# A selective scan in a four-layer network: products written over the states, inputs loaded four units ahead, and doubled pieces one unit earlier

## The chip, the cores and the metric

The kernel runs on one core of a Trainium2 chip. The metric is the device time of one execution in microseconds; the median of some runs is compared. A difference of a few tenths of a per cent is near the limit of what such a comparison can tell.

## What is computed

The network has four layers, each added to its input: a deformable convolution, an edge filter with a 1x1 convolution, a two-way WKV recurrence, and a selective state-space layer (Mamba-like). The change is in the last one. Cut to what matters, for x of 2 x 192 x 96 x 96 (L = 9216 positions), 384 channels d and 16 states n:

```python
x_in, z = split(x_norm @ W_in.T)                 # 384 channels each
u = silu(causal_conv4(x_in) + conv_b)
dt, B, C = split(W_x @ u)                        # 12, 16, 16 rows
delta = softplus(W_dt @ dt + 2 * b_dt)
for t in range(L):                               # for each channel d and state n
    h = exp(delta[t] * A) * h + (delta[t] * u[t]) * B[t]
    y[t] = sum_n(h * C[t])
out = x + W_out @ ((y + D * u) * silu(z))
```

## The kernel before

The last layer is `layer3`. It cuts the 9216 positions of each of the two images into steps ("stages" here): 17 of 511 positions and two of 265 and 264, which are the first two of the first image and the last two of the second. So there are 38 stages. A stage is 12 units, numbered q = 0 to 11; a unit k is a quarter of 128 channels, and its four tiles of 128 partitions hold 8 channels x 16 states each. Everything is float32.

A unit goes through these steps, each a nested function:

- `load` (L2441): SyncE's DMA brings delta * u of the unit's channels, spread over the 16 states, from a DRAM tile `ud` into a buffer `bu` of 128 x 4 x 512. There are four such buffers. `start_of` (L2449, ScalarE) writes the state from the unit's last stage into column 0.
- `times_b` (L2456, GpSimd) multiplies `bu` by B, in place.
- `steps_of` (L2466, TensorE) spreads delta over the states into PSUM banks `da`, of which there are five; `decay` (L2480, ScalarE) takes the four exponentials in place.
- `scan` (L2489, VectorE) runs four scans over the positions, from `da` and `bu` into a tile `h` (three buffers).
- `keep` (L2496, ScalarE) saves the last column of `h`.
- `times_c` (L2513, VectorE) multiplies three of the four tiles of `h` by C, which is in PSUM, into a tile `hc`; `times_c_aside` (L2524, GpSimd) does the fourth into `hp`. Both have three buffers.
- `sum_of` (L2537, TensorE) sums over the states into a bank `acc`; the first unit of each four starts it with `skip` (L2531). After four units `gate` (L2550, VectorE) multiplies by silu(z).

The rest of the work for other stages is cut into pieces by generators, and the loop calls `go` to run the next piece: `early` for the stage after next (21 pieces: two of loading and normalizing; then the six projections, L2344, and three convolutions, L2364, each one piece on TensorE and one copy or activation on ScalarE; then the silu), `late` for the next stage (B, C, delta and the stores to `ud`, L2427, after GpSimd's `du`, L2425) and `output` for the one before. All their matmuls write one PSUM bank, `pe`.

The order on TensorE, VectorE, ScalarE and GpSimd is as written in the loop; SyncE's DMAs are put in order by the scheduler. Within unit k the order is: if q is in `AHEAD`, two pieces; the sum of unit k-2; the scan of k; the load of k+3; the decay matmuls of k+1; one piece of `BEHIND`; the exponentials of k+1; another piece; the product with C; GpSimd's product with C of unit k-1 and its product with B of unit k+2; the first column of k+3; the saved column of k. The tables that say where pieces stand:

```python
AHEAD = {1: "late", 7: "early", 8: "early", 9: "early"}
BEHIND = {0: "late", 1: "late", 2: "late", 3: "out", 4: "out", 5: "early", 6: "early",
          7: "early", 8: "early", 9: "early", 10: "early"}
```

Two or one further pieces are run in units 3, 4, 5, 6, 7 and 11.

Of the kernel before, what the change touches and what calls it, by code (L numbers as in the profile page):

```python
# [6 lines left out]
F32 = mybir.dt.float32  # L7
I32 = mybir.dt.int32
AF = mybir.ActivationFunctionType
ALU = mybir.AluOpType  # L10
# [8 lines left out]
P = 128  # L19
# [44 lines left out]
class Net:  # L64
# [2113 lines left out]
    def layer3(self, x, out, stats):  # L2178
# [3 lines left out]
        nc, tc, ins = self.nc, self.tc, self.ins  # L2182
        TM = 511
# [8 lines left out]
        with ExitStack() as ctx:  # L2192
            wp = ctx.enter_context(tc.tile_pool(name="w3", bufs=1))
            s1 = ctx.enter_context(tc.tile_pool(name="l3s", bufs=1))
            sb = ctx.enter_context(tc.tile_pool(name="l3", bufs=2))
            s3 = ctx.enter_context(tc.tile_pool(name="l3h", bufs=3))
            sc = ctx.enter_context(tc.tile_pool(name="l3c", bufs=4))
            dr = ctx.enter_context(tc.tile_pool(name="l3d", bufs=2, space=DRAM))
# [100 lines left out]
            steps = []  # L2299
# [6 lines left out]
            got = {}  # L2306
# [126 lines left out]
            def where(k):  # L2433
                return k // NQ, k % NQ, k % NQ // NV, k % NV

            def load(k):
                s, q, i, v = where(k)
                T = steps[s][2]
                t = sc.tile([P, 4, TM + 1], F32, name="bu")[:, :, : T + 1]
                one = got[s]["ud"][i, v]  # L2440
                nc.sync.dma_start(  # L2441
                    out=t[:, :, 1:],
                    in_=bass.AP(one.tensor, one.offset, [[0, NST], [4 * T, 8], [1, 4 * T]]),
                )
                got[s]["bu", q] = t

            def start_of(k):
                s, q, _, _ = where(k)
                nc.scalar.copy(  # L2449
                    got[s]["bu", q][:, :, 0], none if steps[s][1] == 0 else state[:, q]  # L2450
                )
# [24 lines left out]
            def decay(k):  # L2476
                s, q, _, _ = where(k)
                for r in range(4):
                    da = got[s]["da", q][r][:, 1:]
                    nc.scalar.activation(  # L2480
                        da, da, AF.Exp, scale=nA[:, 4 * q + r : 4 * q + r + 1]
                    )

            def scan(k):
                s, q, _, _ = where(k)
                h = s3.tile([P, 4, TM + 1], F32, name="h")[:, :, : steps[s][2] + 1]
                bu = got[s]["bu", q]
                for r in range(4):
                    nc.vector.tensor_tensor_scan(  # L2489
                        h[:, r], got[s]["da", q][r], bu[:, r], 0.0, ALU.mult, ALU.add  # L2490
                    )
                got[s]["h", q] = h
# [5 lines left out]
            def rows_c(s):  # L2498
                cc = ps.tile([P, TM], F32, name="cc")[:, : steps[s][2]]
                nc.tensor.matmul(  # L2500
                    cc,
                    pick.rearrange("p n e -> p (n e)"),
                    got[s]["xd"][:NST],
                    start=True,
                    stop=True,
                )
                got[s]["cc"] = cc

            def times_c(k):
                s, q, _, _ = where(k)  # L2510
                T = steps[s][2]
                hc = s3.tile([P, 3, TM], F32, name="hc")[:, :, :T]
                nc.vector.tensor_tensor(  # L2513
                    hc,
                    got[s]["h", q][:, :3, 1:],
                    got[s]["cc"].unsqueeze(1).to_broadcast([P, 3, T]),
                    ALU.mult,
                )
                got[s]["hc", q] = hc

            def times_c_aside(k):
                s, q, _, _ = where(k)
                hp = s3.tile([P, TM], F32, name="hp")[:, : steps[s][2]]
                nc.gpsimd.tensor_tensor(hp, got[s]["h", q][:, 3, 1:], got[s]["cs"], ALU.mult)  # L2524
                got[s]["hp", q] = hp

            def sum_of(k):
                s, q, i, v = where(k)
                if v == 0:
                    acc = ps.tile([P, TM], F32, name="acc")[:, : steps[s][2]]  # L2530
                    nc.tensor.matmul(  # L2531
                        acc, skip[:, i], got[s]["us"][:, i], start=True, stop=False
                    )
                    got[s]["acc"] = acc
                acc = got[s]["acc"]
                for r in range(4):
                    nc.tensor.matmul(  # L2537
                        acc[32 * r : 32 * r + 32],
                        gather[:, v],
                        got[s]["hc", q][:, r] if r < 3 else got[s]["hp", q],  # L2540
                        start=False,
                        stop=v == NV - 1,
                        tile_position=(0, 32 * r),
                    )

            def gate(k):
                s, q, i, v = where(k)
                if i == 0:
                    got[s]["y"] = s1.tile([P, ND, TM], F32, name="y")[:, :, : steps[s][2]]
                nc.vector.tensor_tensor(  # L2550
                    got[s]["y"][:, i], got[s]["acc"], got[s]["zs"][:, i], ALU.mult
                )

            def output(s):
                b, t0, T = steps[s]
                y = got[s]["y"]
                xr = s1.tile([CH, 2, TM], F32, name="xr")[:, :, :T]
                nc.sync.dma_start(out=xr, in_=halves(x[b])[:, :, t0 : t0 + T])
                for m in range(2):
                    pe = bank(T)  # L2560
                    for d in range(ND):
                        nc.tensor.matmul(
                            pe[:CH],
                            w_out[:, d, m * CH : (m + 1) * CH],
                            y[:, d],
                            start=d == 0,
                            stop=d == ND - 1,
                        )
                    yield
                    nc.vector.tensor_tensor(xr[:, m], pe[:CH], xr[:, m], ALU.add)  # L2570
                    if m == 1:
                        nc.sync.dma_start(out=halves(out[b])[:, :, t0 : t0 + T], in_=xr)
                    yield
# [4 lines left out]
                        pass  # L2578
            spare.clear()
            nk = ns * NQ  # L2580
            for k in range(3):
                load(k)
                start_of(k)
            for k in range(2):
# [1 line left out]
            rows_c(0)  # L2586
            steps_of(0)
            decay(0)
            AHEAD = {1: "late", 7: "early", 8: "early", 9: "early"}
            BEHIND = {  # L2590
                0: "late",
                1: "late",
# [12 lines left out]
            def go(name):  # L2605
                next(running[name], None)

            for k in range(nk):
                s, q, _, _ = where(k)
                if q == 0 and s + 1 < ns:  # L2610
                    running["late"] = late(s + 1)
                if q == 2 and s:
                    running["out"] = output(s - 1)
                if q == 3 and s + 2 < ns:
                    running["early"] = early(s + 2)
                if q in AHEAD:
                    go(AHEAD[q])
                    go(AHEAD[q])
                if k >= 2:
                    sum_of(k - 2)  # L2620
                if q == 0 and s:
                    rows_c(s)
                scan(k)
                if k + 3 < nk:
                    load(k + 3)
                if q in (4, 5):
                    go("out")
                if k + 1 < nk:
                    steps_of(k + 1)
                if q in BEHIND:  # L2630
                    go(BEHIND[q])
                if k + 1 < nk:
                    decay(k + 1)
                if q in BEHIND and BEHIND[q] != "out":
                    go(BEHIND[q])
                if q == 3:
                    go("late")
                    go("early")
                    go("late")
                times_c(k)  # L2640
                if q == 4:
                    go("late")
                if k >= 2 and (k - 2) % NV == NV - 1:
                    gate(k - 2)
                if q in (6, 7):
                    go("late")
                if q in (4, 11):
                    go("early")
                if k:
                    times_c_aside(k - 1)  # L2650
                if k + 2 < nk:
                    times_b(k + 2)
                if q == 4:
                    go("late")
                if k + 3 < nk:
                    start_of(k + 3)
                keep(k)
            sum_of(nk - 2)
            times_c_aside(nk - 1)
# [97 lines left out]
```

## Time and profile before

| | |
|---|---|
| median of 3 runs | 10140.82 us (10130.94 to 10147.6) |
| profiled execution | 10135.06 us, its span 10133.3 us |
| last layer's scans | from 7009.46 us to the end |
| busy from 7143 to 10040 us (2897 us) | TensorE 2666, VectorE 2701, ScalarE 1860, GpSimd 2664 us |
| granted TensorE clock, DMA engines' busy share there | 0.91, 0.80 (177 GB/s) |

Times in the profile are microseconds unless marked ns. A group's row gives the line, the engine, the operation, output and inputs by the program's names, shapes, the number, then the busy time and the mean ns of one, then the idle time of the engine just before them and what ended it. A row of waits gives who waited for whom, the total, the number and the longest. PE is TensorE, DVE VectorE, ACT ScalarE, POOL GpSimd, SP SyncE. A float32 matmul stands as two records.

### The profile page before, as it was taken

To read this page: it belongs to the slowest core of one execution; us is meant where nothing else is said; L and a number is where in the kernel's file an instruction comes from. 1 tells how busy PE (TensorE), PEld (TensorE's weight loads), DVE (VectorE), ACT (ScalarE), POOL (GpSimd) and SP (SyncE) were. 2 spreads that over 40 slices of the span, in tenths; PEclk is the share of its full clock that TensorE was granted. 3 is DMA by queue.
4 is the path that set the end of the run, shared out by engine and by line. 5 is a ranking of instruction groups with operands and counts; after the bars stand their busy time and mean duration, and the time that the engine had idled before them with its cause. 6 is when DMAs were issued, how large, how long until landed. Compare 5 with 4: busy or idle time off the path is not lost. (4 is left out here: it accounts for less than half of the span.)

```text
span 10133.3 us, 222497 instructions
## 1 busy us (share of the span) xinstructions
PE 9017.0 (89%) x87686; PEld 5301.1 (52%) x87686; DVE 8276.5 (82%) x8874; ACT 6078.5 (60%) x11850; POOL 7002.5 (69%) x5653
## 2 busy tenths in 40 slices
PE   4799999999979999999979777787999999999998
PEld 3578878877768877788853222223222222222223
DVE  5788878888768887777756789885899999999998
ACT  0366666666657766677721169664666666666665
POOL 1466676666666666666630258774899999999998
PEclk8899999999989999999989888987999999999998
DMA  8455555555424455455545344443788878788876
GB/s 147 96 135 136 140 135 138 136 136 135 126 72 136 137 144 143 138 137 139 137 117 159 122 141 164 125 128 80 173 178 180 178 178 180 178 178 176 180 177 150
DMA packets 878318, 1465.18 MB, mean 145 GB/s; under 512 B 251745, under 2 KB 682405, under 8 KB 877189
## 3 DMA queue, kind: packets, MB, share of 16 engines
q1 hardware_dynamic: 663276, 1264.09, 49.1%
q0 software_dynamic: 105152, 133.19, 5.7%
q10 hardware_dynamic: 108840, 53.57, 2.1%
q8 instruction: 701, 11.49, 0.5%
q14 instruction: 349, 2.85, 0.1%
HBM read 871.06 MB, written 381.46 MB: 124 GB/s over the span
## 5 line engine op out<-in xcount | busy, mean ns | idle before, releaser
L616 DVE TENSOR_TENSOR sp<-h 128x2304 f32<-128x2304 f32 x790 | 2183.5, 2796 | 34.4 <-ACT h L595 34.4
L2489 DVE TENSOR_TENSOR_SCAN h<-da,bu 128x512 f32<-128x512 f32 (+2 forms) x1824 | 1981.2, 1147 | 239.7 <-ACT da L2480 189.7
L2456 POOL TENSOR_TENSOR bu<-bu,bs 128x2044 f32<-128x2044 f32 (+2 forms) x456 | 1960.0, 4298 | 175.9 <-DMA bu<-ud 127.9
L640 ACT COPY st<-pt 128x512 f32<-128x512 f32 (+1 forms) x2370 | 1214.0, 515 | 1090.0 <-PE pt L632 1017.8
L632 PE MATMUL pt<-ident,sp 128*128 128x128 f32 x14220 | 1677.0, 276 | 84.0 <-DVE sp L616 39.0
L638 DVE COPY st<-pt 128x512 f32<-128x512 f32 x1580 | 1060.3, 687 | 760.2 <-PE pt L632 748.4
L632 PEld LDWEIGHTS pt<-ident,sp 128*128 128x128 f32 x14220 | 1567.9, 142 | 166.1 <-issue 95.5
L586 POOL TENSOR_TENSOR h<-u,step 128x1152 f32<-128x1152 f32 (+1 forms) x474 | 1106.9, 2354 | 628.5 <-DVE u L559 436.9
L604 POOL DMA_DIRECT2D xw<-xp_d x2500 | 1391.0, 619 | 153.9 <-PE pt L683 53.4
L2480 ACT ACTIVATE da<-da,nA 128x511 f32<-128x511 f32 (+2 forms) x1824 | 1063.6, 639 | 583.2 <-PE da L2466 577.2
L683 PE MATMUL pt<-st,xw 64*32 64x288 f32 (+1 forms) x30000 | 1107.7, 370 | 169.1 <-DVE st L638 92.1
L709 ACT COPY val<-pt 128x288 f32<-128x288 f32 (+1 forms) x3000 | 958.7, 404 | 306.3 <-PE pt L683 285.6
L811 PEld LDWEIGHTS pf<-main,wd 126*64 126x64 f32 x17064 | 913.9, 140 | 155.6 <-issue 148.4
L811 PE MATMUL pf<-main,wd 126*64 126x128 f32 (+1 forms) x17064 | 986.5, 274 | 9.6 <-DMA far_m<-val 9.2
L2466 PE MATMUL da<-dl,spread 32*128 32x511 f32 (+2 forms) x3648 | 888.2, 650 | 17.5 <-DVE h L2489 17.4
L683 PEld LDWEIGHTS pt<-st,xw 64*32 64x32 f32 x30000 | 547.7, 106 | 594.7 <-DVE st L638 167.6
L2513 DVE TENSOR_TENSOR hc<-h,cc 128x1533 f32<-128x1533 f32 (+2 forms) x456 | 750.7, 1646 | 0.0
L832 PE MATMUL pf<-more,wl 118*64 118x144 f32 (+5 forms) x11592 | 732.9, 277 | 2.5 <-DMA more<-far_l 2.4
L832 PEld LDWEIGHTS pf<-more,wl 118*64 118x64 f32 (+1 forms) x11592 | 665.7, 137 | 69.7 <-issue 62.7
L2466 PEld LDWEIGHTS da<-dl,spread 32*128 32x128 f32 x3648 | 281.2, 194 | 599.7 <-DVE h L2489 370.2
L2524 POOL TENSOR_TENSOR hp<-h,cs 128x511 f32<-128x511 f32 (+2 forms) x456 | 552.7, 1212 | 47.5 <-DVE h L2489 35.6
L2344 PE MATMUL pe<-xn,sb_w_in 96*128 96x511 f32 (+2 forms) x864 | 479.7, 683 | 91.5 <-ACT zs L2359 38.7
(360 smaller groups left out, 13089.2 us busy)
## 6 DMA issues: line engine op xcount, KB each, us to landing
bu<-ud SPq DMA_DIRECT2D x408, 1022.0 KB
main<-val SPq DMA_DIRECT2D x2016, 91.1 KB
far_l<-val SPq DMA_DIRECT2D x288, 324.0 KB
xw<-xp_d POOLq DMA_DIRECT2D x2500, 26.0 KB, 3.1
far_m<-val SPq DMA_DIRECT2D x288, 162.0 KB
half_d<-hv SPq DMA_DIRECT2D x54, 768.0 KB
hv<-half_d SPq DMA_DIRECT2D x54, 768.0 KB
more<-far_l SPq DMA_DIRECT2D x576, 60.8 KB
```

The source lines that it names most:

```text
L586: nc.gpsimd.tensor_tensor(hs, u[:, :, 8 * KK * l : 8 * KK * l + n].unsqueeze(3).to_broadcast([P, 2, n, WS]), con["step"].unsqueeze(1).unsq ...
L604: nc.gpsimd.dma_start(out=xw[e * WN : (e + 1) * WN, i], in_=xp_d[y : y + WS, x : x + WS, e * CM // 2 : e * CM // 2 + XW],)
L616: nc.vector.tensor_tensor(sp.rearrange("p s (y x) -> p s y x", x=WS), hy.unsqueeze(3).to_broadcast([P, n, WS, WS]), hx.unsqueeze(2).to_bro ...
L632: nc.tensor.transpose(pt[:, q], sp[:, 2 * (q0 + q) : 2 * (q0 + q) + 2].rearrange("p e w -> p (e w)"), self.ident,)
L640: nc.scalar.copy(st[:, q0 : q0 + m], pt[:, :m])
L683: nc.tensor.matmul(to, xw[e * WN : (e + 1) * WN, win, g * CG : g * CG + 32], sts[pair][e * WN : (e + 1) * WN].rearrange("p s (r c) -> p s ...
L811: nc.tensor.matmul(place(cv, m, 2 - t // 3, 2 - t % 3, None, 0), con["wd"][:, cv, t, m * CO : (m + 1) * CO], blocks(took, 1, rows), start= ...
L832: nc.tensor.matmul(place(cv, m, 2 * cv if alone else 1 - cv, 2 - t, h, 1 - alone,), con["wl"][lanes, slot, t, m * CO : (m + 1) * CO], bloc ...
L2456: nc.gpsimd.tensor_tensor(bu, bu, got[s]["bs"].unsqueeze(1).to_broadcast([P, 4, steps[s][2]]), ALU.mult)
L2466: nc.tensor.matmul(das[r][:, 1:], spread[at, v].rearrange("p n e -> p (n e)"), got[s]["dl"][at, i], start=True, stop=True, tile_position=( ...
L2480: nc.scalar.activation(da, da, AF.Exp, scale=nA[:, 4 * q + r : 4 * q + r + 1])
L2489: nc.vector.tensor_tensor_scan(h[:, r], got[s]["da", q][r], bu[:, r], 0.0, ALU.mult, ALU.add)
```

## The change

Three edits in `layer3`:

- Both products with C are written over the states in `h`: column t of the output takes the place of column t of a row whose states stand in columns 1 to T, so each product is shifted by one. `hc` and `hp` are gone, the sum reads `h`, and `h` has four buffers instead of three.
- `bu` has five buffers instead of four, in a pool of its own; the load and the first column of unit k+4, not k+3, are issued in unit k, and four instead of three are issued before the loop.
- The two pieces ahead of the sum stand in units 6, 7 and 8 instead of 7, 8 and 9.

Lines below the new pool's are numbered one higher, those below the products fewer by one.

```diff
+            s5 = ctx.enter_context(tc.tile_pool(name="l3b", bufs=5))
...
-                t = sc.tile([P, 4, TM + 1], F32, name="bu")[:, :, : T + 1]
+                t = s5.tile([P, 4, TM + 1], F32, name="bu")[:, :, : T + 1]
...
-                h = s3.tile([P, 4, TM + 1], F32, name="h")[:, :, : steps[s][2] + 1]
+                h = sc.tile([P, 4, TM + 1], F32, name="h")[:, :, : steps[s][2] + 1]
...
             def times_c(k):
-                hc = s3.tile([P, 3, TM], F32, name="hc")[:, :, :T]
+                h = got[s]["h", q]
                 nc.vector.tensor_tensor(
-                    hc,
-                    got[s]["h", q][:, :3, 1:],
+                    h[:, :3, :T],
+                    h[:, :3, 1:],
                     got[s]["cc"].unsqueeze(1).to_broadcast([P, 3, T]),
                     ALU.mult,
                 )
-                got[s]["hc", q] = hc
 
             def times_c_aside(k):
-                hp = s3.tile([P, TM], F32, name="hp")[:, : steps[s][2]]
-                nc.gpsimd.tensor_tensor(hp, got[s]["h", q][:, 3, 1:], got[s]["cs"], ALU.mult)
-                got[s]["hp", q] = hp
+                h = got[s]["h", q][:, 3]
+                nc.gpsimd.tensor_tensor(h[:, : steps[s][2]], h[:, 1:], got[s]["cs"], ALU.mult)
...
-                        got[s]["hc", q][:, r] if r < 3 else got[s]["hp", q],
+                        got[s]["h", q][:, r, : steps[s][2]],
...
-            for k in range(3):
+            for k in range(4):
                 load(k)
                 start_of(k)
...
-            AHEAD = {1: "late", 7: "early", 8: "early", 9: "early"}
+            AHEAD = {1: "late", 6: "early", 7: "early", 8: "early"}
...
-                if k + 3 < nk:
-                    load(k + 3)
+                if k + 4 < nk:
+                    load(k + 4)
...
-                if k + 3 < nk:
-                    start_of(k + 3)
+                if k + 4 < nk:
+                    start_of(k + 4)
```

## The prediction

> Units of a stage are counted 0 to 11 here (q in the code), so the title's units seven to nine are q = 6, 7, 8. "Pieces" are the steps of the generators `early`, `late` and `output`; piece 5 is the second projection of `early`.
>
> **What bounds the kernel now.** I read first the page's groups, then one full stage (units 0 to 11 whose first scan starts at 8586.94 us; the next stage's starts at 8671.68, so it took 84.74 us), grouped by shape on VectorE and GpSimd:
>
> ```profile
> L2489 DVE TENSOR_TENSOR_SCAN h<-da,bu 128x512 f32<-128x512 f32 x48 | 54.7, 1202 | 4.8 <-ACT da L2480 4.7
> L2513 DVE TENSOR_TENSOR hc<-h,cc 128x1533 f32<-128x1533 f32 x13 | 22.5, 1728 | 0.0
> L2550 DVE TENSOR_TENSOR y<-acc,zs 128x511 f32<-128x511 f32 x3 | 2.0, 682 | 0.8 <-PE acc L2537 0.8
> L2456 POOL TENSOR_TENSOR bu<-bu,bs 128x2044 f32<-128x2044 f32 x12 | 54.2, 4515 | 4.6 <-DMA bu<-ud 4.6
> ```
>
> VectorE idles only 4.8 + 0.8 = 5.6 us in the stage, and nearly all of it waits for the decays (`da`), which TensorE and ScalarE make; GpSimd idles 4.6 us for the loads of `bu`. The products with C wait for nothing (0.0). Over the whole layer the table of waits says how much of GpSimd's lateness reaches VectorE:
>
> ```profile
> DVE h L2489 <- ACT da L2480: 189.7, 174, 22.5
> POOL bu L2456 <- DMA bu<-ud: 119.4, 68, 5.7
> DVE h L2489 <- POOL bu L2456: 42.9, 26, 4.8
> ```
>
> So 119.4 us of load waits become at most 42.9 us on the path. What makes the decays late is read from the chain of waits between 8620 and 8700 us, which is units 5 to 9 of that stage (start, length, what):
>
> ```profile
> 8627.69 3.75 PE pe L2344 x4
> 8631.44 1.70 PE acc L2531 x2
> 8633.14 1.24 PE acc L2537 x8
> 8634.38 1.11 PE da L2466 x8
> 8635.49 2.37 ACT da L2480 x4
> 8637.86 0.52 ACT xi L2352
> 8638.43 1.99 PE pe L2344 x4
> ...
> 8649.53 2.37 ACT da L2480 x4
> 8651.90 0.53 ACT zs L2359
> 8652.43 0.04 issue
> 8652.47 3.69 PE pe L2364 x8
> 8656.17 0.99 PE acc L2537 x8
> ```
>
> From 8627.69 on the chain is TensorE and ScalarE, no longer VectorE. A doubled piece is a link of its own: its matmul uses the one bank `pe`, so it waits for the copy of the piece before it (8637.86), and that copy stands behind the four exponentials. Note the first row: four matmuls in 3.75 us, while the same four take 1.99 later. The table of stretches tells why (length, TensorE busy, granted clock, then DMA):
>
> ```profile
> 8626.79:8630.20 3.41, 2.85 (x4) 0.50 0.49 128
> 8630.21:8633.61 3.40, 3.40 (x8) 0.50 0.83 216
> 8633.63:8637.03 3.40, 3.40 (x20) 1.00 0.33 75
> 8456.13:8459.53 3.40, 2.73 (x9) 1.00 0.41 120
> 8459.55:8462.95 3.40, 3.40 (x5) 0.50 0.74 187
> 8462.96:8466.36 3.40, 3.40 (x19) 1.00 0.82 206
> ```
>
> The clock is at half in unit 5 of each stage and changes only on a grid of 3.41 us. A half-clock stretch that TensorE filled (3.40) was followed by full clock, here and in another stage at 8459.55; one with 0.56 us of idle (2.85) was followed by a second half-clock stretch.
>
> **The change, part by part.**
>
> *Products written over the states.* The same 12 products a stage on VectorE, the same 12 on GpSimd, same shapes; two pools go. An in-place product with a PSUM operand stands in the trace: `xr` (L2570), 655 ns for 511 columns, against 682 ns for `y` (L2550), which is not in place. GpSimd's product with B (L2456) is in place: 4515 ns for 2044, 1129 for 511, against 1266 for `hp` today. So I take 0. Bounds: 12 x -0.03 = -0.3 us a stage; upward the in-place L2419, 2.09 us for the 1533 elements of a 1.73 us product, a different operation: +0.36 us x 12 = +4.3 us. It also adds no wait: the state saved by ScalarE is the column T, which no product overwrites, and `h` gets a fourth buffer, so the scan of unit k overwrites unit k-4, whose sum TensorE issued two units before. The waits that go (for `hc` and `hp` buffers) cost 0.0 today.
>
> *Five buffers, loads four ahead.* A load is still released by the scan of unit k-1, but it is for unit k+4, so it has one unit (6.1 us or more) longer to land. It stays one place behind on SyncE's queue relative to the `ud` stores: today units 10 and 11 wait there behind the store that waits for GpSimd's `du`, after the change only 11. GpSimd's waits at the products of units 10 and 11 (1.53, 1.91 and 0.19 us here, longest 5.7) go. On the path that is between 0 and the 42.9 us above; but where unit 11 was late, the wait of 1.41 us in the next unit 1 (the silu and its table loads) shrank: 42.9 - 26 x 1.41 = 6. I take 6 to 12, about 0.3 us a stage. Cover: GpSimd's own work, 79 us a stage, must stay below the stage; it does.
>
> *Doubled pieces one unit earlier.* All 21 pieces of `early` stay; those of units 6 to 8 move. Today the doubled ones are the projections 7 and 11 and the convolution 15 (L2364, 3.69); afterwards the projections 5, 9 and 13.
> Removed: in unit 9 the convolution follows the decay matmuls at once, without waiting for exponentials and copy: 2.37 + 0.53 + 0.04 = 2.94 us off the chain.
> Added: in unit 6 TensorE, done with the first projection at 8631.44, must wait for its copy (end 8632.11, start 8632.15: 0.71 us, as in 8637.86 to 8638.43) and then do piece 5 ahead of the sums and the decay matmuls for unit 7. VectorE has no slack there: unit 7's scan waits for its decay already. Two prices:
> - clock back at 8633.62 as today: piece 5 does 1.47 us at half and 0.98 at full rate, 2.45; the skip and sum after it now run at full rate (0.86 + 0.99 for 1.70 + 1.24, -1.09). 0.71 + 2.45 - 1.09 = 2.07, net -0.87 us a stage.
> - half clock for one stretch more: piece 5 takes 4 x 0.855 = 3.42, the skip 1.70, the sum 0.99 (-0.25): 0.71 + 3.42 - 0.25 = 3.88, net +0.94 us.
> The stretch 8630.21 to 8633.61 gets an idle of 0.71; it would be busy for 2.7 us, less than the 2.85 after which the clock stayed at half. So I take the second price for a stage that lies like this one, and the first where the grid falls so that one stretch holds all of the first projection.
>
> The Trainium skill, "TensorE: Matmul & The Clock Gate", section "HAM oscillation — how this bites in real kernels", says that idle gaps are harmless below about 3.4 us. By that rule the 0.71 us costs no clock, and the sum would be the first price in every stage, 10103 us. This trace differs from it: the idle of the stretch at 8626.79 is 0.56 us, and the clock was at half for it and the next one. [...]
>
> **The sum.** 33 full stages lie between 7142.77 and 9949.52: 85.05 us each, of which I put 0.3 to late loads. A stage like this one goes to 84.74 + 0.94 = 85.7, one with the clock back early to 83.9. Which of them comes is set by the grid: 25 of its steps are 25 x 3.413 = 85.33 us. Unit 5's half clock began at 8541.46, 8626.79, 8712.13, 8797.46 and 8882.79, always 85.33 apart though the stages differ. A stage of 85.7 slides 0.4 us against the grid each time until the early case comes, and one of 83.9 slides back; the mean settles near 85.33. 33 x (85.33 - 85.05) = +9 us. The four half-length stages I leave at 0 (at the prices of a full stage, 4 x -0.87 to 4 x +0.94). The profiled execution is 10135.06 us (span 10133.3 and 1.8 around it), so it becomes 10144; the median of the three runs lies 5.8 above it: 10150. That is no change: 0.2% (20 us) is about what a measurement of this kernel can tell.
>
> **Rivals.**
> *Faster, the clock comes back in time.* The 0.7 us does not hold the clock down. Then every full stage is near 83.9: 33 x 1.15 = -38, 10103. For it: other idle gaps, 1.06 us each in units 7 to 9, leave the clock at 1.0. Against it: those begin at full clock, and the one row that begins at half with a gap stayed at half.
> *Slower, unit 6 is the new late unit.* The half clock holds for one stretch more in every full stage and nothing slides back: 85.7 to 86.1 (late loads unchanged), 33 x 0.65 to 1.05 = +21 to +35, 10162 to 10176. It decides if in nearly every stage unit 7's scan starts over 9.5 us after unit 6's (6.50 here). An in-place product at L2419's price would add to it: in units 0 to 6, where VectorE is the bound, 7 x 0.36 x 33 = +83.
> *It does nothing on the path:* loads early, products the same, links exchanged at par: 10141, inside the forecast's case.
>
> **How the numbers follow.** No change, 0.37: the grid's mean and the exchange at par. Faster 0.31: it needs a clock that recovers, or late loads at more than I take; low end 10085, the early clock with 18 of the 42.9 us on top. Slower 0.32: the extra stretch; the high end, 10190, is the slower case with a part of the in-place bound. The forecast's own range is 10121 to 10161.
>
> **What would show it.** Right: no wait of L2457 for `bu`; scan before unit 7 waiting about 3 us for `da`, none before 10 and 11; the gap before the gate gone; half-clock stretches in unit 5 reaching 10.2 us; stages near 85.3. Wrong: L2514 above 1.75 us (in-place price), unit 7 waiting below 2.3 us (clock back), or TensorE no longer on the chain in units 7 to 9.

## The result, and the profile after

| | before | after |
|---|---|---|
| median | 10141.74 us (10128.45 to 10154.08, 18 runs) | 10160.17 us (10142.56 to 10166.25, 18 runs) |
| ratio after / before | | 1.0016, 95% interval 1.0009 to 1.0022 |
| profiled execution, its span | 10135.06, 10133.3 us | 10163.15, 10161.2 us |
| first scan of the last layer | 7009.46 us | 7020.69 us |
| first scan to the end of the span | 3123.83 us | 3140.55 us |
| mean of the 33 full stages | 85.05 us | 85.51 us |

The forecast was 10150 us and no change beyond 0.2%. The time is 18 us longer by the medians, 0.16%, with an interval whose upper end just passes 0.2%. It is a near thing: the forecast's own range ends at 10161, and 8 of the 18 runs lie above that. The two profiled executions differ by 28 us, but 11.2 of these lie before the layer's first scan, where of the change only the fourth load stands (over all kernels of this case that point lies between 7000.8 and 7020.7 us). The layer itself is 16.7 us longer, 33 x 0.46 = 15.2 of it in full stages.

The same groups as before, for the stage that starts at 8609.29 us and takes 85.50 us (output and inputs, shapes, number, busy us, mean ns, idle before and what ended it):

```profile
L2490 DVE TENSOR_TENSOR_SCAN h<-da,bu 128x512 f32<-128x512 f32 x49 | 56.0, 1203 | 7.0 <-ACT da L2481 7.0
L2514 DVE TENSOR_TENSOR h<-h,cc 128x1533 f32<-128x1533 f32 x13 | 22.5, 1727 | 0.0
L2549 DVE TENSOR_TENSOR y<-acc,zs 128x511 f32<-128x511 f32 x3 | 2.0, 683 | 0.0
L2420 DVE SCALAR_TENSOR_TENSOR du<-ln,du 128x1533 f32<-128x1533 f32 x1 | 1.7, 1747 | 0.0
...
L2457 POOL TENSOR_TENSOR bu<-bu,bs 128x2044 f32<-128x2044 f32 x12 | 54.2, 4518 | 1.2 <-DMA bu<-ud 1.2
```

The in-place product takes 1727 ns (1728 before): no price. The gap before the gate is gone (0.8 to 0.0), and GpSimd's wait for loads is down from 4.6 to 1.2. VectorE's wait for the decays grew from 4.7 to 7.0. Over the layer the waits say the same:

```profile
DVE h L2490 <- ACT da L2481: 283.8, 166, 22.6
...
POOL ln L2422 <- DVE du L2420: 137.2, 34, 4.3
...
POOL bu L2457 <- DMA bu<-ud: 59.2, 34, 7.0
...
DVE h L2490 <- POOL bu L2457: 14.9, 8, 4.5
```

VectorE waits 94 us more for `da` (283.8 against 189.7) and 28 us less for `bu` (14.9 against 42.9). The chain of waits of the same stage shows where the new wait is made (start, length, what; units 5 to 7):

```profile
8649.40 3.76 PE pe L2345 x4
8653.16 0.02 issue
8653.18 0.02 ACTq L2353
8653.20 0.04 issue
8653.24 0.59 ACT xi L2353
8653.83 0.04 issue
8653.88 3.78 PE pe L2345 x4
8657.65 1.29 PE acc L2530 x2
8658.94 0.99 PE acc L2536 x8
8659.94 1.11 PE da L2467 x8
8661.05 2.37 ACT da L2481 x4
```

TensorE ends the first projection at 8653.16, waits 0.72 us for its copy, and then does the second one in 3.78 us, all at half clock. And the table of stretches (length, then the busy time of TensorE, its weight loads, VectorE, ScalarE and GpSimd, each with its number of instructions, then granted clock, DMA share and GB/s):

```profile
8648.16:8651.57 3.41, 3.18 (x5) 1.17 (x4) 3.41 (x5) 0.82 (x2) 3.41 (x2) 0.50 0.52 136
8651.58:8654.98 3.40, 2.67 (x4) 0.59 (x3) 3.40 (x4) 0.78 (x3) 3.40 (x2) 0.50 0.90 216
8654.99:8658.40 3.41, 3.41 (x6) 1.25 (x4) 2.64 (x2) 0.58 (x1) 3.41 (x3) 0.50 0.43 100
8658.41:8661.81 3.40, 3.40 (x20) 0.96 (x19) 0.02 (x1) 0.78 (x2) 3.40 (x1) 1.00 0.02 3
```

The stretch with the gap (2.67 busy of 3.40) was followed by a third one at half clock; that one was filled (3.41), and the clock came back. Unit 5's half clock is 10.24 us long in 32 of the 33 full stages (6.83 in 24 of them before), and from stage 5 to 26, counted from 0, it begins every 85.33 us: 8562.83, 8648.16, 8733.50, 8818.83. These are 25 steps of the 3.41 us on which the clock changes (the grid). A stage whose length stays at a whole number of such steps is called locked below.

### The profile page after: what moved, and what is told of

The parts are those of the page before. It is cut to its first block, busy times and chain, and to the rows that moved or that the text cites. A ratio compares the mean times of both kernels' runs of the same rounds, so it can differ in the third digit from the quotient of the medians.

```text
span 10161.2 us, 221966 instructions
## 1 busy us (share of the span) xinstructions
PE 9094.1 (89%) x87686; PEld 5330.0 (52%) x87686; DVE 8244.7 (81%) x8874; ACT 6084.1 (60%) x11850; POOL 6984.1 (69%) x5653
## 5 line engine op out<-in xcount | busy, mean ns | idle before, releaser
L2490 DVE TENSOR_TENSOR_SCAN h<-da,bu 128x512 f32<-128x512 f32 (+2 forms) x1824 | 1981.5, 1148 | 307.4 <-ACT da L2481 283.8
L2457 POOL TENSOR_TENSOR bu<-bu,bs 128x2044 f32<-128x2044 f32 (+2 forms) x456 | 1960.3, 4299 | 68.0 <-DMA bu<-ud 67.7
L2467 PE MATMUL da<-dl,spread 32*128 32x511 f32 (+2 forms) x3648 | 908.9, 645 | 13.3 <-DVE h L2490 13.3
L2514 DVE TENSOR_TENSOR h<-h,cc 128x1533 f32<-128x1533 f32 (+2 forms) x456 | 750.9, 1647 | 0.6 <-PE da L2467 0.6
L2345 PE MATMUL pe<-xn,sb_w_in 96*128 96x511 f32 (+2 forms) x864 | 544.7, 764 | 117.0 <-ACT xi L2353 64.6
L2524 POOL TENSOR_TENSOR h<-h,cs 128x511 f32<-128x511 f32 (+2 forms) x456 | 553.3, 1213 | 102.4 <-DVE h L2490 56.7
```

The source lines that it names most:

```text
L2457: nc.gpsimd.tensor_tensor(bu, bu, got[s]["bs"].unsqueeze(1).to_broadcast([P, 4, steps[s][2]]), ALU.mult)
L2467: nc.tensor.matmul(das[r][:, 1:], spread[at, v].rearrange("p n e -> p (n e)"), got[s]["dl"][at, i], start=True, stop=True, tile_position=( ...
L2490: nc.vector.tensor_tensor_scan(h[:, r], got[s]["da", q][r], bu[:, r], 0.0, ALU.mult, ALU.add)
```

## The experiments

All ratios are to the kernel before, with 95% intervals. "Stage" is the mean of the 33 full stages of the profiled execution, which need not be the median one: for the sum first in unit 6 the five runs go from 10073 to 10113 us, and the fastest was profiled.

| what runs | median us | ratio | stage us |
|---|---|---|---|
| doubled pieces in 6 to 8, nothing else | 10196.67 | 1.0052 (1.0038 to 1.0066) | 86.41 |
| in place, five buffers, four ahead | 10137.93 | 0.9995 (0.9986 to 1.0004) | 84.86 |
| in place only | 10146.12 | 1.0003 (0.9994 to 1.0012) | 85.04 |
| after, sum first | 10043.33 | 0.9900 (0.9885 to 0.9915) | 82.13 |
| after, sum first in unit 6 | 10100.24 | 0.9956 (0.9942 to 0.9969) | 83.55 |
| after, sum first in units 7, 8 | 10140.07 | 0.9997 (0.9988 to 1.0006) | 84.97 |
| after, sum first, pieces in 7 to 9 | 10100.40 | 0.9956 (0.9942 to 0.9970) | 84.08 |
| after, sum first, pieces in 5 to 7 | 10155.42 | 1.0005 (0.9996 to 1.0014) | 85.51 |
| after, sum first, pieces in 5, 7, 8 | 10135.20 | 0.9992 (0.9984 to 1.0001) | 84.98 |
| before, pieces in 6 to 8, sum first | 10169.50 | 1.0028 (1.0018 to 1.0038) | 86.27 |
| after, one VectorE product more, from SBUF | 10271.85 | 1.0123 (1.0108 to 1.0139) | 88.82 |
| after, one VectorE product more, from PSUM | 10157.52 | 1.0012 (1.0004 to 1.0021) | 85.49 |

### The change taken apart

**The doubled pieces alone.**

```diff
-            AHEAD = {1: "late", 7: "early", 8: "early", 9: "early"}
+            AHEAD = {1: "late", 6: "early", 7: "early", 8: "early"}
```

> Only the doubled pieces move to units 6, 7 and 8; products, buffers and loads as before. Theory (the exchange of links holds the half clock for a third stretch, and stages settle on 25 grid steps): unit 7's scan waits about 4 us, half-clock stretches of 10.2 us in most stages, stages near 85.3 to 85.7 with the late loads still there, 10145 to 10170 us. Rival (the products over the states or the new buffers cost the time): this kernel is at the time of the one before, 10141, or below it, and unit 7 waits below 1 us.

Measured 10196.67, above the range: unit 7's scan waits 4.36 us, as the theory has it, but the stages do not hold at 85.33; they run from 85.1 to 90.2. The exchange of links (the doubled piece that leaves unit 9's chain and the one that enters unit 6's) costs time, and alone it costs three times what the whole change does.

**Buffers and products, pieces where they were.** The changed kernel with the line above put back.

> Products over the states, five buffers and loads four ahead, with the doubled pieces left in units 7, 8 and 9. Theory: GpSimd's load waits in units 10 and 11 go, worth 6 to 12 us on the path (0.2 to 0.3 us a stage), the half clock stays at two stretches or less, 10125 to 10140 us. Rival (earlier loads or in-place products lengthen VectorE's or GpSimd's rows, or the start of unit 0): 10150 or above.

Measured 10137.93, 4 to 5 us below before and not told from no change. GpSimd's waits in units 10 and 11 are gone. But VectorE waits more for the decays than before (231.5 against 189.7 us) and 14 of the 33 full stages take 85.3: what the loads gave seems to be mostly taken back by TensorE.

**Products over the states alone.** Loads three ahead, four buffers, pieces in 7 to 9.

```diff
-                    hc,
-                    got[s]["h", q][:, :3, 1:],
+                    h[:, :3, :T],
+                    h[:, :3, 1:],
```

> Only the products with C are written over the states; loads three ahead in four buffers, doubled pieces in units 7, 8 and 9. Theory: the rows of the products keep their 1.73 and 1.27 us, 10141 within 10. Rival (an in-place product is dearer, 0.1 us or more each): 12 x 33 x 0.1 = +40 us or more.

Measured 10146.12, the products 1726 and 1267 ns. The price is 0, as taken.

So the parts add as -5 (buffers and products), +54 (pieces), and +18 together, not +49: with the pieces moved the buffers and products are worth 36 us, without that 5. Part of the 36 is a row I had not costed. `du` (L2419 before) takes 2272 ns on average in full stages before, 2077 with the pieces alone, and 1747 after. The added product below shows why.

### The gap in the half clock

**The sum ahead of the doubled pieces.** TensorE then has the sum of unit k-2 to do while ScalarE copies the piece before.

```diff
+                if k >= 2 and q != 1:
+                    sum_of(k - 2)
                 if q in AHEAD:
                     go(AHEAD[q])
                     go(AHEAD[q])
-                if k >= 2:
+                if k >= 2 and q == 1:
                     sum_of(k - 2)
```

> The changed kernel, but with the sum of unit k-2 ahead of the doubled pieces in units 6, 7 and 8, so that TensorE does the sum while ScalarE copies the piece before. Theory (the 0.7 us of idle at half clock in unit 6 holds the clock down): the idle goes, the half clock ends after 6.8 us, unit 7 waits below 2.5 us, stages near 84 or below, 10085 to 10110 us. Rival (the clock is held by what runs, not by the gap: the decay products with 32 rows, or the length of the link in unit 6 whatever its idle): the half clock stays at 10.2 us in most stages, and the stages stay on 85.33, 10150 to 10165.

Measured 10043.33: 1.0% faster than before and better than the theory's range. The chain and the stretches of one stage:

```profile
8585.16 3.75 PE pe L2345 x4
8588.91 1.70 PE acc L2530 x2
8590.61 1.43 PE acc L2536 x8
8592.04 1.91 PE pe L2345 x4
8593.95 1.11 PE da L2467 x8
```

```profile
8584.64:8588.05 3.41, 2.89 (x4) 1.37 (x5) 3.41 (x4) 0.56 (x1) 3.41 (x1) 0.50 0.64 161
8588.06:8591.46 3.40, 3.40 (x11) 0.67 (x10) 3.40 (x4) 0.77 (x3) 3.40 (x2) 0.50 0.93 215
8591.47:8594.87 3.40, 3.40 (x20) 0.99 (x12) 1.92 (x2) 0.58 (x1) 3.40 (x3) 1.00 0.24 59
```

The gap of 0.72 us is gone, the second stretch is full, the clock is back at 8591.47, and the second projection takes 1.91 us in place of 3.78. Unit 7 waits 2.14 us (4.25), units 8 and 9 next to nothing (0.86 and 0.79).

**In unit 6 alone, and in units 7 and 8 alone.** The same edit under `q in (6,)` and `q in (7, 8)`.

> The changed kernel with the sum ahead of the doubled pieces in unit 6 alone. Theory (the idle of 0.7 us in the half clock of unit 6 is what costs a third stretch): the half clock of unit 5 ends after 6.8 us, unit 7 waits about 2.2 us instead of 4.3, units 8 and 9 wait 0.8 as before; 2.1 us a stage less on the path, stages near 83.4, 10085 to 10105 us. Rival (the gain of the version with all three sums ahead came from the gaps in units 7 and 8, which are removed there too): 10130 to 10160.

> The changed kernel with the sum ahead of the doubled pieces in units 7 and 8, not in 6. Theory (those are full-clock gaps on the chain, each worth its own 0.8 us): unit 7 still waits 4.3 us, half clock still 10.2 us, units 8 and 9 wait about 0; 1.6 us a stage less at most, 10105 to 10125, but if the grid of the half clock sets the stage, as it did at 25 steps, part of it is given back and the time is 10130 to 10160.

In unit 6 alone: 10100.24, 60 us less than after; unit 5's half clock is 6.83 or 3.41 us long in the stages of the middle, and units 8 and 9 keep their 0.79 and 0.80. In units 7 and 8 alone: 10140.07, 20 us less than after, although 1.6 us a stage of gaps went (33 x 1.6 = 53); unit 7 still waits, and most full stages stand at 84.7 to 85.3. Both together give 117, more than 60 + 20: with unit 6's gap in place, the clock takes most of the gain back. With that gap filled, the two gaps in units 7 and 8 are worth 57 (10100.24 to 10043.33), about the 53 that they measure.

The profiles allow a count, from TensorE's records and the granted clock, over all half-clock stretches of 3.41 us from the layer's first scan on:

| kernel | over 0.5 us of idle, then half clock again | under 0.2 us of idle, then full clock |
|---|---|---|
| before | 15 of 17 | 89 of 147 |
| changed | 52 of 54 | 111 of 136 |
| changed, sum first | 16 of 18 | 83 of 135 |

So a gap of half a microsecond nearly always went with a further stretch at half clock, but a filled stretch brought the clock back only in three to four cases of five. The two filled stretches that the prediction showed were not enough to see that. The Trainium skill, "TensorE: Matmul & The Clock Gate", section "Part 1: The HAM clock gate (the "warmup" mystery)", has the clock come back after at least one busy window of about 3.4 us; the rows above agree in that one filled stretch can do, and that many needed more. The rule that the prediction weighed is about losing the clock, and could not be used for getting it back. For losing it, it is not enough here either: in the 33 full stages of the changed kernel TensorE's longest gap is 2.32 us, and the clock falls 100 times.

### Does the grid hold the stage?

**One VectorE product more.**

```diff
+                if q == 2:
+                    nc.vector.tensor_tensor(idle, idle, idle, ALU.mult)
```

> The changed kernel with one more VectorE product, 264 columns on a scratch tile that nothing reads, about 0.4 us, in unit 2 of each stage, where VectorE is the bound. If the grid holds the stages at 25 steps: stages stay at 85.33, the layer no more than 5 us longer, 10155 to 10168. If the stage is simply the sum of its rows: 33 x 0.4 = +13 us, 10173 or so. If the lock breaks upward, as with the pieces alone: stages over 86, +25 us or more.

Measured 10271.85: no test of the grid, for the product did not take 0.4 us but 4.17 on average (0.52 to 6.27; mean of the 31 between 7160 and 9900 us). One of them on VectorE's timeline, and GpSimd's product beside it:

```profile
8585.70 4.61 DVE L2643 TENSOR_TENSOR idle<-idle 128x264 f32<-128x264 f32 x1
...
8585.52 4.50 POOL L2459 TENSOR_TENSOR bu<-bu,bs 128x2044 f32<-128x2044 f32 x1
```

It started 0.18 us after GpSimd's and ended 0.29 after it: it stood still until GpSimd was done. Over the 33 full stages the added products take 135 us (4.09 each), which covers the 112 us. The Trainium skill, "SBUF — State Buffer", section "SBUF: two separate sides", calls the port pair of VectorE and GpSimd an exclusive lock, for a VectorE operation with two SBUF inputs beside a GpSimd operation that reads SBUF; this run agrees. It also explains `du`, which reads two SBUF tiles: before, it begins in 22 of 34 stages inside a GpSimd product and stops for the rest of it (at 8025.67 us, 1.43 us of the product were left, and `du` took 3.05 us, 1.62 more; at 0.65 us left it took 2.27, again 1.62 more). After, GpSimd is ahead, waits for `du` (the 137.2 us above), and `du` takes 1.75 us in every stage.

**The same with one operand in PSUM.**

```diff
+                if q == 2:
+                    nc.vector.tensor_tensor(idle, got[s]["cc"][:, :264], idle, ALU.mult)
```

> The changed kernel with one more VectorE product of 264 columns in unit 2 of each stage, but with one operand in PSUM (the rows of C), so that it doesn't wait for GpSimd's product as the one with both operands in SBUF did (4.17 us instead of 0.4); nothing reads its result. If the grid of the clock holds the stages at 25 steps: product 0.40 us, stages stay at 85.33, 10155 to 10168 us. If a stage is the sum of its rows: +13 us against the changed kernel, about 10173. If the lock breaks upward: stages over 86, 10185 or more.

```profile
L2643 DVE TENSOR_TENSOR idle<-cc,idle 128x264 f32<-128x264 f32 x32 | 13.6, 426 | 0.0
```

426 ns each, 14 us in the full stages, and the time is 10157.52, 3 us below the changed kernel. From stage 5 to 25 the stages are 85.33 each, without and with the product. Unit 2 is 0.34 us longer, units 1 and 6 together 0.35 shorter: VectorE's added work comes out of its waits for TensorE, whose clock sets the stage. The grid holds. With the sum first the stages 5 to 25 are 81.97 on average and unit 5's half clock begins every 81.92 us, 24 steps, though single stages go from 80.8 to 83.0; whether that kernel too would absorb added work was not tried.

### Other places, and the buffers again

**Sum first, pieces in 7 to 9.** 

> The changed kernel with the sum ahead of the doubled pieces, and these in units 7, 8 and 9 as in the kernel before. Theory (the place of the pieces matters little once TensorE has the sum to do during the copy): waits of units 8 to 10 and of the gate go, 0.7 to 1.0 us each, stages near 82 to 83, 10040 to 10090 us. Rival (moving the pieces one unit earlier is worth something by itself, the link of 2.9 us that it takes out of unit 9): 10100 or above.

Measured 10100.40, at the rival's edge. With the sum first, the places 6 to 8 are worth 57 us against 7 to 9: the gate's wait goes, but unit 9 waits 1.82 us and unit 10 0.91, where with 6 to 8 it is 0.07 and 0.

**Sum first, pieces in 5 to 7.** 

> The changed kernel with the sum ahead of the doubled pieces and these in units 5, 6 and 7. If the remaining 2.1 us of wait before unit 7 is only the work that stands together at half clock in units 5 and 6, pairs earlier spread it, TensorE has more to do in unit 4 to 5, and the stage falls below 81.5: below 10040. Rival (unit 5's pair comes before the half clock ends, and its copy waits for GpSimd's ln, which reads the same tile): unit 6 waits 2 us or more, 10045 or above.

**Sum first, pieces in 5, 7 and 8.** 

> As before it, with the doubled pieces in units 5, 7 and 8, so that unit 6 has a single piece. If the half clock's work is spread by this: unit 7 waits below 1 us, unit 6 not over 1, 10010 to 10040 us. Rival (the wait only moves from unit 7 to unit 6): 10040 to 10060.

10155.42 and 10135.20. The first is the rival's time, the second is outside both ranges. Unit 6 now waits 4.4 us in both, and unit 7 still 1.6 and 0.5: a pair in unit 5 does not spread the work. The reason is not the one in the expectation, since the table of waits has no copy that waits for GpSimd. The chain of the kernel with 5 to 7, in its unit 5:

```profile
8638.28 0.59 DVE xr L2569
8638.88 0.14 issue
8639.01 3.74 PE pe L2345 x4
8642.75 1.97 PE da L2467 x8
8644.72 1.91 PE pe L2345 x4
```

The first projection starts when the product `xr` of unit 5 has read the bank `pe` for the output. A pair there adds a projection behind that point and starts nothing earlier. The stages of this kernel alternate, most near 83.9 and 86.8 us; two of them make 170.7, and 50 steps are 170.67, so a lock need not be of one stage.

**Sum first without the buffers.** The kernel before, with the pieces in 6 to 8 and the sum ahead of them.

> The kernel before with the doubled pieces in units 6, 7 and 8 and the sum ahead of them; products into tiles of their own, four buffers, loads three ahead. Theory (GpSimd's load waits cost more once the stage is not held on the grid of the clock): GpSimd's late products show on the path, 0.4 to 1.5 us a stage, 10055 to 10095 us. Rival (buffers and loads are worth as little here as alone, 5 us): 10040 to 10052.

Measured 10169.50, well above both ranges. Buffers and products, worth 5 us with the pieces in 7 to 9 and 36 with the pieces moved, are worth 126 here; the products alone gave nothing above. In that kernel VectorE waits for GpSimd's late products, mostly before unit 11 (2.41 us a stage):

```profile
DVE h L2489 <- ACT da L2480: 171.7, 109, 22.4
...
POOL bu L2456 <- DMA bu<-ud: 149.8, 83, 8.3
...
DVE h L2489 <- POOL bu L2456: 107.0, 73, 5.8
```

GpSimd's waits for loads are not much longer than before (149.8 against 127.9 over the whole execution). But VectorE, which then waits less for TensorE and ScalarE (171.7 against 189.7), waits 107.0 us for GpSimd's product where it waited 42.9, and the kernel is no faster than before. That the loads are the whole reason for the 126 is argued from these waits; no run has the loads four ahead without the products over the states. Neither half of the good version is worth much without the other.

## Why the prediction was right, and where its steps were off

The mechanism is the one that was forecast: the doubled piece in unit 6 holds the clock at half for a third stretch, and the stages settle on 25 steps of the grid. That the sum came within 10 us is partly luck, since sizes that were off cancel, as the steps show.

*In-place products, 0.* Right; shown alone. The upper bound was made from the wrong cause: `du`'s 2.09 us was its wait for GpSimd's port, not a price of writing in place.

*The exchange of links.* Removed: units 9 and 10 shrank by 1.86 and 1.08 us, 2.94 as predicted. The match is partly luck: with the pieces alone it is 1.86 and 0.80, so some 0.28 of it belongs to the loads. Added: in the example stages, from the end of the first projection to the decay matmuls it is 6.78 us against 2.94, 3.84 more (second price: 3.88); unit 6 as a whole grew by 4.02. Here two errors cancel: the second projection takes 3.78, not 3.42, and the skip after it 1.29, not 1.70, because the clock comes back during it. But the half-clock price was the right one of the two, and the clock did stay at half for the third stretch. The figure of "about 3 us" for unit 7's wait contradicted this price: 0.26 before and 3.88 more make 4.1, and it measured 4.25.

*Late loads, 0.3 us a stage.* The waits in units 10 and 11 went as said. One remains in 29 of the 33 full stages, at the product of the next stage's unit 0, whose load comes after the `ud` stores (1.8 us, 7.0 at most); so the sign "no wait of L2457 for `bu`" did not come, 59.2 of 119.4 us are still there. The credit depends on what else is late: 5 us alone, 36 with the pieces, 126 with the sum first, each with the products over the states. A single figure for it could not be right.

*Missed.* `du` is 0.5 us shorter because GpSimd no longer holds the port; unit 4 shrank by 0.53, 17 us over the full stages that the forecast did not count on; how much of it the grid lets through was not tried. Net over the units: +4.02 - 2.94 - 0.53 and -0.09 elsewhere = +0.46.

*The grid.* The sum put 33 x (85.33 - 85.05) = +9; it is +15.2. From stage 5 to 25 the mean is 85.33. The rest is outside the lock: stages 2 to 4 take 87.7, 86.3 and 85.6, and stages 26 to 28 85.8, 87.9 and 85.7, together 7 us over 85.33. The step's picture, stages of 85.7 that slide until one of 83.9 comes, is not what happens: with the same 10.24 us of half clock every time, 85.2, 85.3 and 85.5 repeat. So the value of the mean came out right and the way to it did not. The term that was mis-sized is the stages before and after the lock, which I left out.

*The rivals.* Faster by a clock that comes back: the clock does come back earlier if the gap is filled, and then the time is 10100 (unit 6 alone), close to the 10103 of that rival, though by other means, since that rival still counted the 0.71 us of the gap; and the changed kernel does not fill it. Slower in every stage with late loads unchanged: that is the kernel with the pieces alone, at 10197 still above its 10162 to 10176.

## What to carry to other kernels

Where an engine's clock falls and returns on a grid, price a gap by the stretch that it lies in: 0.7 us of idle in a half-clock stretch cost 60 us here (24 are the idle itself), while two gaps at full clock, 1.6 us a stage, gave 20 when they were filled. The order matters too: once the first gap was filled, the same two gave 57. Put independent work, like the sum, between two steps that share a buffer. Before crediting an edit, ask which engine is late behind it: the same buffers and products were worth 5 or 126 us.

## What the runs showed of the hardware that I had not expected

- A stage can lock to the clock's grid: 85.33 us with or without 0.43 us more of work on VectorE.
- A VectorE product with both inputs in SBUF that begins inside a GpSimd product waits for the rest of it: 4.17 us on average for 264 columns, against 0.43 with one input in PSUM.
- The clock often falls after a stretch that shows no idle: in the changed kernel 88 of 115 falls followed a stretch with less than 0.2 us of it. In the one before 8648.16 the last four decay matmuls stand as 4.51 us of busy time, where they usually take 1.14, so the records seem to hold waiting; before the fall at 8626.79 in the kernel before they stand as 4.52. What makes the clock fall stays open.
